# The first pair's first layer as 64-row halves from a list of slots, its setup and loads in another order

## The chip, the cores and the metric

The kernel runs on one core of a Trainium2 chip. The core has a matrix engine (PE, with weight loads shown apart as PEld), a vector engine (DVE), a scalar engine (ACT) and a general engine (POOL); SP only issues transfers. Each engine works through a queue of its own in the order in which the program issued its instructions, and semaphores make one engine wait for another. PE writes its products to PSUM, which has eight banks of 128 rows by 512 numbers. The metric is the device time of one execution in microseconds (us).

## The reference

It is a mixture of experts over 8 batches of 512 tokens with 256 features; all numbers are 32 bits wide.

```python
nx = layer_norm(x, ln_gamma, ln_beta)
weights = softmax((nx @ Wq) @ (ctx @ Wk)^T / 16)          # 64 prototypes of each batch
evidence = weights @ (ctx @ Wv)
combined = concat([nx, evidence, anchor])                 # 768 features; anchor is one row of a batch
router_probs = softmax(combined @ router_W + router_b)    # 3 experts
h = silu(combined @ e_w1 + e_b1)                          # 3 experts of 512
routed = sum over experts of (h @ e_w2 + e_b2) * router_probs
g = sigmoid(silu(combined @ gate_w1 + gate_b1) @ gate_w2 + gate_b2)
out = x + g * (routed @ out_w + out_b)
```

## The kernel before, in words

The batches are worked in four pairs (`j` = 0 to 3). The two batches of a pair and the two halves of the 256 features make 2 by 2 blocks, and the kernel forms block products by Strassen's scheme in Winograd's form: seven products in the place of eight. The sums of inputs are the tile `T` (`combine_x`), the sums of weights are `ws`, `w2s` and `gw2s` (`combine_weights`, `combine_second`, `combine_gate`, on POOL).

**Setup.** Context, weights and x are loaded by SP, ACT and POOL. PE transposes, joins the key weights, forms the values, and then the scores. DVE subtracts the maxima, ACT takes the exponential (line 679), DVE sums and divides and turns the weights (`turn_weights`). `value_weights` multiplies the values by an expert's evidence weights (`ps_vw`); ACT copies them out and `value_differences` subtracts. `anchor_rows` multiplies the anchors by an expert's anchor weights, in 32-column pieces; `anchor_columns` adds the biases (`abias`). `second_bias` does the same for the second layer's bias.

**First layer.** The first layer has seven groups of two 128-feature chunks: group 0 is the gate, groups 1 and 2 are expert 0, 3 and 4 expert 1, 5 and 6 expert 2. A group has the products P1 to P7 (`nx_operands`, line 881), collected in PSUM sums called U, Z and Y (and W for the gate). To these sums come evidence products of only 64 rows, since a batch has 64 prototypes; two of them, one on the upper and one on the lower 64 rows of PE, run side by side. A chunk is made in steps: ACT copies a sum out (`keep_part`, line 876), DVE adds another (`add`, line 873), ACT applies silu with the anchor's bias (line 867), and DVE multiplies by the router's probability (`weigh_chunk`, line 924, or subtracts, line 921).

**Order.** All queues are in program order (`manual_schedule(engines=None)`, line 1426). `gate_layer` issues P1, P5, P2, P6, P3 and P7 of the gate, with other steps put between. In pairs 1 to 3 `half_layers` then reads the list `SLOTS`. Each line is a slot: two half products, the first on the upper 64 rows and the second on the lower, and behind the bar the steps of the other engines that are issued after them. So every product is split in two halves that stand in different slots; `half_product` adds a semaphore wait where a bank goes from one half to the other. `HOME` gives the bank of each sum. In the steps, k is a copy out of PSUM, a an add, s a silu, w a weighing, df a difference, each with two digits for the chunk and the group behind the dot; st, nm and lg are statistics, normalization and router part of the next pair; r is the router with the spreading of its probabilities (`pb`, a round trip through memory); g is a gate difference.

In pair 0 the first layer runs in another way: `expert_layer` issues whole 128-row products of two groups at a time, and `evidence` issues the 64-row products in four blocks, behind the gate and behind each expert. Between them the lists `within` put steps that pair 0 alone has: the anchors of experts 1 and 2, the combined weights of experts 1 and 2, and the second layer's product of `e_w2` and `out_w`. For that, `transpose_second` turns one expert's `e_w2` (DVE) in scratch tiles that earlier held setup data, `second_layer` multiplies it by `out_w`, and `combine_second` forms its sums on POOL. `outputs` then does the gate's second layer, the expert sums and the stores, and prepares the next pair.

The helper `product` (line 809) records nearly all products, so PE's instructions are told apart by their tiles: `ps_u`, `ps_z`, `ps_y` and `ps_w` are the sums above; `ps_gu`, `ps_gz` and `ps_gy` are the gate's second layer. A 32-bit product is two PE instructions in the trace.

## Time and profile before

| | |
|---|---|
| median of 3 runs (lowest to highest) | 459.16 us (458.97 to 459.51) |
| profiled execution: its time, its span | 458.83 us, 457.0 us |
| PE busy | 451.6 us (99%) |
| DVE, ACT, POOL busy | 364.0, 214.6, 100.3 us |
| granted PE clock | 1.000 |
| PE in pair 0: first score product | starts at 19.30 us |
| PE in pair 0: first gate product of the outputs | starts at 95.36 us |

The span reaches from the first to the last instruction, and times inside the profile count from its start. A line of the timeline gives start, duration, engine, line of the program, operation, output and input tile, their shapes, the number of instructions, and in brackets the idle time of the engine just before with what seems to have ended it. Products overlap on PE, so that the distance of two starts says more than a duration. Where the engine named in the brackets had long been done, another one ended the wait.

### The profile page before, as it was taken

How to read it: one execution, taken by the hardware profiler on the slowest of the kernel's cores; microseconds unless marked ns; L12 is line 12 of the kernel's file. 1: busy time of each engine (PE TensorE's matmuls, PEld its weight loads, DVE VectorE, ACT ScalarE, POOL GpSimd, SP SyncE). 2: the span in 40 equal slices, each digit the busy share in tenths (PEclk: the TensorE clock that was granted, in tenths of full speed). 3: DMA queues.
4: the chain of work that ended last, by engine and by line, in shares of the span. 5: the costliest groups of instructions: out<-in, count | busy, mean ns of one | idle time of the engine just before them, and what ended most of it. 6: DMA issues, size and time to landing. Idle time of an engine off the chain costs nothing.

```text
span 457.0 us, 5304 instructions
## 1 busy us (share of the span) xinstructions
PE 451.6 (99%) x1711; PEld 212.8 (47%) x1711; DVE 364.0 (80%) x679; ACT 214.6 (47%) x373; POOL 100.3 (22%) x148
## 2 busy tenths in 40 slices
PE   9999999999999999999999999999999999999996
PEld 7534555444444444444444444444444444444445
DVE  2888979969699899479689999578869746677983
ACT  3545683655221585467221576468220456558000
POOL 5367715001072300001062300001044300000010
PEclk9999999999999999999999999999999999999999
DMA  8985587302011387303011377102011390000014
GB/s 266 384 163 125 94 241 123 91 0 46 7 23 25 58 241 129 81 0 48 6 23 23 48 226 126 19 0 47 6 23 23 55 223 3 0 0 1 0 17 75
DMA packets 119346, 35.30 MB, mean 77 GB/s; under 512 B 105980, under 2 KB 116280, under 8 KB 118808
## 3 DMA queue, kind: packets, MB, share of 16 engines
q1 hardware_dynamic: 115312, 27.02, 29.2%
q0 software_dynamic: 2080, 7.16, 4.7%
q10 hardware_dynamic: 1928, 0.80, 0.7%
q8 instruction: 13, 0.21, 0.2%
q14 instruction: 13, 0.11, 0.1%
HBM read 27.56 MB, written 7.39 MB: 76 GB/s over the span
## 4 chain that ended last, share of the span: by engine, by line
PE 97%; POOL 1%; issue 0%; DVE 0%; ACT 0%; POOLq 0%
PE ps_u L809 45%; PE ps_z L809 19%; PE ps_y L809 14%; PE ps_vw L782 5%; PE ps_gu L809 3%; PE ps_w2o L510 2%; PE ps_gz L809 2%; PE ps_s L660 1%; PE ps_tokens L809 1%; PE ps_wake L307 1%; PE ps_v L347 1%; PE ps_gy L809 1%; PE ps_m L347 1%; PE pt_ctx L326 0%; PE pt_x L590 0%; PE ps_kq L360 0%
## 5 line engine op out<-in xcount | busy, mean ns | idle before, releaser
L809 PE MATMUL ps_u<-nxT,w 64*128 64x512 f32 (+1 forms) x184 | 86.8, 591 | 0.0
L924 DVE TENSOR_TENSOR h<-h,pb 128x512 f32<-128x512 f32 x96 | 63.4, 698 | 14.8 <-ACT h L867 12.2
L809 PE MATMUL ps_u<-h,w2o 128*128 128x512 f32 x144 | 64.2, 595 | 0.0
L867 ACT ACTIVATE h<-h,abias 128x512 f32<-128x512 f32 x72 | 49.3, 718 | 24.4 <-DVE h L873 24.2
L809 PE MATMUL ps_z<-wT,vw 64*128 64x512 f32 x104 | 51.6, 593 | 0.0
L1331 POOL TENSOR_TENSOR yb<-yb,xb 128x512 f32<-128x512 f32 x14 | 17.7, 1267 | 148.9 <-DVE yb L1330 131.7
L809 PE MATMUL ps_z<-T,ws 64*128 64x512 f32 (+1 forms) x92 | 46.4, 590 | 0.0
L809 PE MATMUL ps_z<-nxT,ws 64*128 64x512 f32 (+1 forms) x92 | 45.9, 590 | 0.0
L809 PEld LDWEIGHTS ps_u<-nxT,w 64*128 64x128 f32 (+1 forms) x184 | 33.2, 188 | 26.9 <-issue 24.5
L809 PE MATMUL ps_y<-nxT,w 64*128 64x512 f32 (+1 forms) x92 | 45.5, 590 | 0.0
L809 PE MATMUL ps_u<-T,ws 64*128 64x512 f32 (+1 forms) x92 | 42.9, 590 | 0.7 <-POOL gg L412 0.7
L809 PE MATMUL ps_z<-h,w2s 128*128 128x512 f32 x96 | 42.5, 592 | 0.0
L809 PE MATMUL ps_u<-T,w 64*128 64x512 f32 (+1 forms) x98 | 42.4, 589 | 0.0
L809 PEld LDWEIGHTS ps_u<-h,w2o 128*128 128x128 f32 x144 | 27.0, 190 | 32.6 <-issue 30.4
L876 ACT COPY h<-ps_u 128x512 f32<-128x512 f32 x48 | 27.9, 582 | 24.1 <-PE ps_u L809 22.0
L1298 DVE TENSOR_TENSOR h<-h,h 128x1024 f32<-128x1024 f32 x24 | 34.3, 1485 | 0.0
L424 POOL DMA_DIRECT2D vrd<-vw x8 | 5.0, 628 | 133.2 <-ACT vw L789 128.9
L809 PEld LDWEIGHTS ps_z<-h,w2s 128*128 128x128 f32 x96 | 18.2, 190 | 23.0 <-issue 22.3
L809 PE MATMUL ps_y<-wT,vw 64*128 64x512 f32 x56 | 28.0, 596 | 0.0
L809 PE MATMUL ps_u<-wT,vw 64*128 64x512 f32 x56 | 27.9, 595 | 0.0
L782 PE MATMUL ps_vw<-w,vT 128*128 128x512 f32 (+1 forms) x64 | 26.9, 543 | 0.0
L873 DVE TENSOR_TENSOR h<-h,ps_u 128x512 f32<-128x512 f32 x24 | 16.1, 684 | 11.2 <-PE ps_u L809 11.1
(224 smaller groups left out, 814.3 us busy)
## 6 DMA issues: line engine op xcount, KB each, us to landing
pb<-pd POOLq DMA_DIRECT2D x4, 1536.0 KB, 6.5
xb<-in_x_dram SPq DMA_DIRECT2D x64, 64.0 KB, 2.4
out_dram<-yb SPq DMA_DIRECT2D x56, 64.0 KB, 2.0
w<-in_L_xcond_e_w_dram SPq DMA_DIRECT2D x6, 512.0 KB, 10.5
x<-in_x_dram SPq DMA_DIRECT2D x24, 128.0 KB, 2.8
xd<-x SPq DMA_DIRECT2D x24, 128.0 KB, 2.4
xg<-xd SPq DMA_DIRECT2D x48, 64.0 KB, 2.3
scr_wa<-in_L_xcond_e_w_dram SPq DMA_DIRECT2D x3, 512.0 KB, 17.4
```

Source lines behind the costliest of these rows:

```text
L307: nc.tensor.matmul(ps_wake[0][:, :P], zeros, zeros, start=True, stop=True)
L347: nc.tensor.matmul(ps, w_sb[:, k, m * P : (m + 1) * P], src[:, k, :], start=(k == 0), stop=(k == KH - 1))
L424: nc.gpsimd.dma_start(S["vrd", j][i].rearrange("e c -> c e"), S["vw", j][row_half(i), R0:])
L510: nc.tensor.matmul(ps[:, d * H : (d + 1) * H], w2T[:, k, (i + d) * P : (i + d + 1) * P], ow_sb[:, k, :], start=(k == 0), stop=(k == KH - 1),)
L782: nc.tensor.matmul(ps, vT[:, k, j * 2 * CT : (j + 1) * 2 * CT], w1[:, KH + k, n0:n1], start=(k == 0), stop=(k == KH - 1),)
L809: return nc.tensor.matmul(ps, lhsT, rhs, start=start, stop=True, skip_group_check=not start)
L867: nc.scalar.activation(h, h if src is None else src, AF.Silu, bias=abias[:, c, 2 * j + i : 2 * j + i + 1])
L873: nc.vector.tensor_tensor(h, h, part, ALU.add)
L876: nc.scalar.copy(chunk(n, i, d), part)
L924: nc.vector.tensor_tensor(h, h, S["pb", j][:, i, :, 2 * q // RC, :], ALU.mult)
L1298: nc.vector.tensor_tensor(d, p, m, ALU.subtract)
L1331: nc.gpsimd.tensor_tensor(yb, yb, S["xb", 2 * j + row][:, i, :], ALU.add)
```

## The change

Pair 0 uses `gate_layer` and `half_layers` like the others, with lists of its own: `SLOTS_0`, `UNITS_0`, `LATE_0` and `HOME_0`. The old way (`expert_layer`, `evidence`, `weigh` and what they call) is gone. In the lists `lp` is the router part of pair 0, `rl` its router logits, `rx` the exponential, `c2` and `cg` combine the weights of expert 2 and of the gate, `lx`, `l1` and `l2` issue loads, and `t` turns half of an expert's `e_w2`.

- The second layer's products stand behind the slots, in six units of half an expert; the transposed halves lie in two tiles, taken in turns. `e_w2` is loaded to tiles of the `xb`, `r11` and `r12` buffers in the place of scratch, and the load of expert 0 is issued in the setup.
- The anchors of all three experts and the second bias are one block of products to one bank (`late_anchors`), with one transpose, between `gate_layer` and the slots.
- `load_first` loads one part at a time: the evidence parts of all experts come ahead of the first parts of experts 1 and 2, and the anchor weights are loaded between.
- The gate's weights are combined before the first transposes of x; those of experts 0 and 1 behind the softmax, held back by a one-element copy on POOL (`wake_t`) that reads the softmax.
- `scores` is split: `exponents` (all behind the products) is issued after the gate's P1 and its copy. All four `combine_x` steps of pair 0 are on DVE. The three `ps_vw` products are inside `gate_layer`; the rest of the softmax is issued behind P7 and before its add.

```diff
-    def load_first(g):
+    def load_first(g, part):
         src, n = (e_w1[g], RH) if g < E else (gate_w1, H)
-        cs = slice(g * RH, g * RH + n)
-        nc.sync.dma_start(w1[:, KH:, cs], rows_of(src[H : 2 * H, :]))
-        nc.sync.dma_start(w1[:, :KH, cs], rows_of(src[:H, :]))
+        lo = part * KH
+        nc.sync.dma_start(
+            w1[:, lo : lo + KH, g * RH : g * RH + n], rows_of(src[part * H : (part + 1) * H, :])
+        )
...
+    def turned(ps, rows_of_k, weights, first):
+        for k in range(KH):
+            w = weights[:, k, :].rearrange("p (c i f) -> p i c f", i=P // QB, f=QB)
+            for i in range(P // QB):
+                dst = ps[i * QB : (i + 1) * QB, first : first + weights.shape[2] // (P // QB)]
+                nc.tensor.matmul(
+                    dst.rearrange("p (c f) -> p c f", f=QB), rows_of_k[:, k, :], w[:, i, :, :],
+                    start=(k == 0), stop=(k == KH - 1),
+                )
...
+    def late_anchors():
+        ps = bank(1, "ps_ar")
+        for g in range(E):
+            turned(ps, condT, wa[g], g * P)
+        turned(ps, b2T, ow_sb, E * P)
+        blocks = work.tile([P, T], F32, tag="yb", name="ar_blocks")
+        n = E * P + KH * QB
+        nc.vector.transpose(blocks[:, :n], ps[:, :n])
+        for g in range(E):
+            ar[g] = blocks[:, g * P : (g + 1) * P]
+        ar["b2"] = blocks[:, E * P : n]
...
+    def second_layer(u):
+        e, i = u // 2, 2 * (u % 2)
+        ps = bank((4, 7, 6, 5)[u % 4], f"ps_w2o_{u}")
+        for d in range(2):
+            for k in range(KH):
+                c = k * H + d * P
+                nc.tensor.matmul(
+                    ps[:, d * H : (d + 1) * H], w2["T"][u % 2][:, c : c + P], ow_sb[:, k, :],
+                    start=(k == 0), stop=(k == KH - 1),
+                )
+        c = e * RC + i
+        nc.scalar.copy(w2o[:, c : c + 2, :].rearrange("p c n -> p (c n)"), ps)
+        if i:
+            combine_second(e)
...
+            if t0 == 0:
+                S["ls", b] = work.tile([P, NT], F32, tag="ls", name=f"ls_{b}")
+            sums = S["ls", b]
         for t in range(t0, t1):
             nc.vector.scalar_tensor_tensor(
                 junk, S["xn", b][:, t, :], 1.0, gg, ALU.mult, ALU.mult, accum_out=sums[:, t : t + 1]
             )
-        if j == 0:
+        if j == 0 and t1 == NT:
...
+        S["ps_s", j] = ps
+    def exponents(j):
+        ps = S.pop(("ps_s", j))
...
+        def run(point):
+            for step in steps.get(point, ()):
+                step()
         for i in range(2):
             for k in range(KH):
                 S["hg", i, k] = hpool.tile([P, T], F32, tag=f"hg{i}{k}", name=f"hg_{2 * j + i}_{k}")
         U[n], Z[n], Y[n] = (bank(i, f"ps_{u}_{j}_{n}") for i, u in ((0, "u"), (2, "z"), (3, "y")))
         nx_product(j, n, 1, True)
         keep_part(n, 0, 0, U[n])
-        if j == 0:
-            anchor_columns(E)
-            anchor_columns(0)
...
+        run(1)
         nx_product(j, n, 5, True)
         keep_part(n, 1, 1, Z[n])
+        run(5)
         nx_product(j, n, 2, True)
         nx_product(j, n, 6)
         keep_part(n, 1, 0, U[n])
-        for step in steps.get("gate early", ()):
-            step()
+        run(6)
         nx_product(j, n, 3)
-        for step in steps.get("gate", ()):
-            step()
+        run(3)
         nx_product(j, n, 7)
+        run("sums")
...
+    SLOTS_0 = (
+        "P1.1 Z.1 |",
+        "Y.1 Z.0 |",
+        "P1.3 P1.1 | lp0.0 a10.0",
+        "Y.0 W.0 | k00.1 lp0.1 s10.0 lp0.2",
+        "P2.1 P1.3 | w11.0",
+        "P4.0 P5.1 | a00.0 k00.3 s11.0 lp0.3 c2",
+        "P6.1 P2.1 | lp1.0 s00.0 lp1.1",
+        "P5.1 Z.2 | a00.1",
+        "U.0 P6.1 | lp1.2 k11.1 lp1.3 cg lx l1 l2 s00.1",
+        "P1.2 P5.2 | rl k10.1",
+        "Y.2 P4.0 |",
+        "P5.2 P1.2 | s01.0",
+        "P2.3 P3.1 | k00.2 k11.2",
+        "P7.1 V.1 | g0 rx",
+        "P2.2 Z.3 | st0.0 st0.1",
+        "P6.2 P7.1 | st0.2 st0.3",
+        "Y.3 P5.3 | a11.1",
+        "P3.1 P6.2 | r s11.1",
+        "P6.3 V.2 | st1.0 k10.2 a10.1",
+        "P5.3 P3.2 | st1.1 s10.1",
+        "U.1 P2.2 | st1.2 k11.3 st1.3",
+        "P3.2 P2.3 | a00.2 dev",
+        "P1.6 P6.3 | g1 a00.3",
+        "P7.2 P3.3 | a10.2",
+        "P4.1 P1.6 | g2",
+        "P2.4 P7.2 | g3 k10.3 nm0.0 k00.6",
+        "P1.5 P4.1 | nm0.1 a11.2 s00.2",
+        "P1.4 V.3 | nm0.2 s01.1 nm0.3 xd0",
+        "P7.3 P1.5 | nm1.0 s00.3 nm1.1 nm1.2 s10.2",
+        "P3.3 P1.4 | nm1.3 xd1 xg w00.1 k00.5",
+        "P6.6 Z.6 | a10.3 k00.4",
+        "P4.2 P7.3 | s11.2 w10.1 w11.1 s10.3",
+        "U.2 P6.6 | a11.3",
+        "P6.5 Z.4 | k10.6 w00.2 s11.3 w01.1",
+        "P6.4 P4.2 | w00.3",
+        "Y.4 P6.5 | s01.2 w10.2",
+        "U.3 P6.4 | w11.2 k10.5 w10.3",
+        "P4.3 P2.4 | k10.4 w11.3",
+        "Y.6 P5.4 | a00.4 w01.2",
+        "P7.5 P4.3 | s00.4 lg0.0",
+        "P5.4 P5.6 | w00.4 s01.3 lg0.1",
+        "P7.4 Z.5 | k11.4 w01.3",
+        "P5.6 P5.5 | lg0.2 lg0.3",
+        "Y.5 P7.4 | lg1.0 k11.6 lg1.1",
+        "P5.5 P7.5 | lg1.2 a11.4",
+        "P2.5 P3.4 | k11.5 lg1.3 s11.4 df.1",
+        "P7.6 V.6 | a11.5 t0",
+        "P2.6 P3.6 | w11.4 s11.5",
+        "U.4 V.5 | df.2 w11.5",
+        "P3.6 P7.6 | df.3",
+        "U.5 P3.5 | a11.6 a10.6 t1",
+        "P4.5 V.4 | s11.6 s10.6 w11.6",
+        "P4.4 P2.5 | w10.6",
+        "U.6 P4.5 | a00.5",
+        "P4.6 P4.4 | s00.5 s01.5",
+        "P3.4 P2.6 | w00.5 s01.4 w01.5",
+        "P3.5 P4.6 | a00.6",
+    )
+    UNITS_0 = (
+        "a10.4 s01.6 s10.4",
+        "t2 a10.5 s00.6",
+        "w01.4 t3 s10.5 xb0 xb1",
+        "w01.6 w00.6 t4",
+        "w10.4 t5",
+        "w10.5",
+    )
+    LATE_0 = ("", "", "df.6 df.4 df.5")
+    HOME_0 = {
+        "U.0": 0, "Z.0": 2, "Y.0": 3, "W.0": 1, "U.1": 4, "Z.1": 5, "Y.1": 6, "U.3": 7, "Z.2": 2,
+        "U.2": 1, "Y.2": 3, "Y.3": 6, "Z.3": 0, "U.6": 5, "Y.4": 3, "U.5": 6, "U.4": 2, "Z.6": 4,
+        "Z.4": 0, "Y.6": 1, "Z.5": 3, "Y.5": 7,
+    }
...
+            "rl": lambda: router_logits(j),
+            "rx": lambda: router_exp(j),
+            "c2": lambda: combine_weights(2),
+            "cg": lambda: combine_gate(),
+            "lx": lambda: [load_x(b) for b in (2, 3)],
+            **{f"l{e}": lambda e=e: load_second(e) for e in range(1, E)},
+            **{f"t{u}": lambda u=u: transpose_second(u) for u in range(2 * E)},
...
+        if not j:
+            for u, tokens in enumerate(UNITS_0):
+                second_layer(u)
+                for token in tokens.split():
+                    step(token)
+        S["late", j] = [lambda t=tokens: [step(x) for x in t.split()] for tokens in late]
...
-        for g in (E, 0):
-            load_first(g)
-            load_anchor(g)
-        for g in (1, 2):
-            load_first(g)
+        load_first(E, 1)
+        load_first(E, 0)
+        load_anchor(E)
+        load_first(0, 1)
+        load_first(0, 0)
+        load_first(1, 1)
+        load_first(2, 1)
+        load_anchor(0)
...
+        combine_weights(E)
         transpose_x(0)
+        late_scratch()
+        load_anchor(1)
+        load_anchor(2)
+        nc.sync.dma_start(ow_sb, rows_of(out_w))
+        load_first(1, 0)
+        load_first(2, 0)
+        nc.sync.dma_start(gw2_sb, rows_of(gate_w2))
+        load_second(0)
...
-        combine_weights(E)
         load_table(AF.Exp)
         combine_x(0, nc.vector, (0, 1))
+        spares(6, 4, 5, 7)
         scores(0)
-        anchor_rows(0)
-        combine_x(0, nc.gpsimd, (2,))
-        router_column()
-        spread_router_bias()
-        combine_weights(0)
-        spread_router_rows(0)
-        value_weights(0, 0, nc.scalar.copy, False)
-        sum_weights(0)
-        softmax(0)
-        value_differences(0, 0)
-        turn_weights(0)
-        late_scratch()
-        load_anchor(1)
-        load_anchor(2)
-        nc.sync.dma_start(ow_sb, rows_of(out_w))
-        nc.sync.dma_start(gw2_sb, rows_of(gate_w2))
-        load_second(0)
+        def begin_softmax():
+            exponents(0)
+            combine_x(0, nc.vector, (2,))
+        def end_softmax():
+            sum_weights(0)
+            softmax(0)
+            nc.gpsimd.tensor_copy(wake_t, S["w", 0][:, 0, 0, 0:1])
+            value_differences(0, 0)
+            turn_weights(0)
+            anchor_columns(E)
+            combine_x(0, nc.vector, (3,))
+            combine_weights(0)
+            router_column()
+            spread_router_bias()
+            spread_router_rows(0)
+            combine_weights(1)
+        def end_setup():
+            value_differences(0, 1)
+            late_anchors()
+            for g in range(E):
+                anchor_columns(g)
+            value_differences(0, 2)
+            second_bias()
...
+            spares(7, 5)
             if j == 0:
+                spares(4, 5, 7)
+                copies = []
+
+                def value_product(g):
+                    value_weights(0, g, lambda *args: copies.append(args), False)
+
+                def copy_values():
+                    nc.scalar.copy(*copies.pop(0))
+
+                put(within, 1, value_product, 0)
+                put(within, 1, begin_softmax)
+                put(within, 5, copy_values)
+                put(within, 6, load_table, AF.Silu)
+                put(within, 3, value_product, 1)
+                put(within, 3, copy_values)
+                put(within, "sums", end_softmax)
+                put(within, 7, value_product, 2)
+                put(within, 7, copy_values)
+                put(within, 7, end_setup)
...
-            if j:
-                half_layers(j)
-            else:
-                for e in range(E):
-                    expert_layer(j, e, within)
+            half_layers(j)
             outputs(j, between)
```

## Prediction

> **What bounds the kernel now.** I read the busy times first, then the chain that ended last, then TensorE's own timeline of the first pair, and only then the queues of the other engines.
>
> ```profile
> span 457.0 us, 5304 instructions
> PE 451.6 (99%) x1711; PEld 212.8 (47%) x1711; DVE 364.0 (80%) x679; ACT 214.6 (47%) x373; POOL 100.3 (22%) x148
> PE 97%; POOL 1%; issue 0%; DVE 0%; ACT 0%; POOLq 0%
> ```
>
> TensorE (PE) is the chain. The clock row is 9 in all 40 slices, so nothing is to be had there. A change helps only if it takes products or gaps out of PE's queue, and it harms as soon as another engine makes PE wait. PE's timeline of the first pair shows what gaps there are:
>
> ```profile
> 25.12 1.02 PE L809 MATMUL ps_y<-nxT,w 128*128 128x512 f32 x2
> 26.82 1.10 PE L809 MATMUL ps_u<-T,ws 128*128 128x512 f32 x2 [0.68 <-POOL gg L412]
> ...
> 30.33 1.02 PE L809 MATMUL ps_u<-nxT,w 128*128 128x512 f32 x2
> 31.29 0.69 PE L809 MATMUL ps_y<-wT,vw 64*128 64x512 f32 x1
> ...
> 31.82 0.59 PE L809 MATMUL ps_y<-wT,vw 64*128 64x512 f32 x1
> ...
> 34.39 0.59 PE L809 MATMUL ps_y<-wT,vw 64*128 64x512 f32 x1
> ...
> 34.92 1.13 PE L809 MATMUL ps_u<-nxT,w 128*128 128x512 f32 x2
> 35.88 1.02 PE L809 MATMUL ps_u<-T,w 128*128 128x512 f32 x2
> ```
>
> Starts matter here, not durations, because products overlap. A full product is two instructions and takes 0.857 us (35.88 to the next start, 36.74); a pair of 64-row halves takes 0.429 an instruction, so 0.857 as well. Halves are therefore no faster in themselves. What costs is the border between the two shapes: 30.33 to 31.29 is 0.96, not 0.857, and 31.29 to 31.82 is 0.53, not 0.43. That is 0.1 on either side, 0.2 a border; 34.39 to 34.92 (0.53) and 34.92 to 35.88 (0.96) say the same of the way back. The first pair goes to halves and back four times: eight borders, 1.6 us. Pairs 1 to 3, which run the list of slots, have two each.
>
> The gap at 26.82 is put down to gg, but no operand of that product (P6 of the gate) is gg. It adds into bank ps_u, which ScalarE (ACT) has to read first, and ACT's queue shows when it did:
>
> ```profile
> 25.13 0.63 ACT L679 ACTIVATE w<-w 128x512 f32<-128x512 f32 x1 [4.00 <-DVE w L678]
> 25.67 0.57 ACT L789 COPY vw<-ps_vw 128x512 f32<-128x512 f32 x1
> 26.14 0.59 ACT L876 COPY hg<-ps_u 128x512 f32<-128x512 f32 x1
> ```
>
> The copy stood behind the softmax's exponential, ended at 26.73, and PE went on at 26.82. P2 was issued out at 25.98, so PE lost 0.84.
>
> **The change, part by part.** Account: PE from the first score product (19.30) to the first gate product of the outputs (95.36), 76.06 us. Work in it: scores 1.73, anchors 0.56 + 1.23, three ps_vw 5.16, 63 products and pairs of halves 54.0, second layer 10.35: 73.0. The rest, 3.0, is borders 1.6, the ACT wait 0.84, and some 0.6 of single gaps (0.25 behind the anchors, 0.19 in the third second-layer block).
>
> *Products.* All 57 first-layer products and evidence pairs stay, now as 57 slots; the 24 second-layer products stay, in six units of 1.72 (half of a 3.45 block). No work goes. Borders fall from eight to two: **-1.2**.
>
> *ACT order.* The copy of ps_u is issued ahead of the exponential, so P6 is free: **-0.84**. What is late next: the copy of ps_z is now behind the exponential. ACT 25.67 + 0.59 = 26.26, and P3 would start at 26.2 to 26.35: **+0.1**.
>
> *Anchors together*, second bias with them, as one block of the same 64 instructions: gap of 0.2 at one place instead of two, **-0.2**.
>
> *Loads on SP, DMAs on POOL.* SP moves load_anchor(0) behind two more weight loads, takes the first-half loads of experts 1 and 2 behind ow_sb, and sends the eight DMAs of load_second(0) at some 19 to 24 instead of 30.5, where SP stood 11.2 us on a scratch tile. DMA is busy to about 26 now; the moved loads of 512 KB are first read at 34 or later: nothing, up to +0.5 if the 64 KB DMAs delay them. POOL combines the gate weights before the router column's two DMAs, which go out at 16, not 14.2; 6.1 us to landing is 22, needed at 30: nothing. The wake copy holds POOL until the softmax is done (27.45); behind it are combine(0) 2.75, gg 1.8, four DMAs 2.15 and combine(1) 2.75: 37.2. P2 of expert 0 reads combine(0) (30.4) in slot 5 at 37; covered.
>
> *Start of the slots.* PE: scores to 21.03, six gate products 5.15, three ps_vw 5.15, anchors 1.8, borders 0.3: slot 1 at **33.5**. DVE: softmax as before to 30.5, then 0.2 + 0.6 + 0.6 + 0.4, then the anchors' transpose at 33.5 (0.65), columns 0.35, difference 0.4, second bias 1.06: its first slot step at **36.1**, in slot 3, where it is listed.
>
> *DVE's ledger.* From 36.1 to the last transpose before unit 5 the lists put on DVE: 21 adds and 23 weighings and 3 differences at 0.60 (28.2), 16 router parts at 0.44 (7.0), router logits 3.93, router 0.85, eight statistics at 0.53 (4.2), eight normalizations (3.1), four gate differences (2.6), six half transposes at 0.74, worked out between 0.30 for 128 columns and 0.71 for 512 (4.4): **54.3**. PE reaches unit 5 at 33.5 + 0.1 + 48.9 + 8.6 = 91.1, so 55.0 are there: **slack 0.7**. Before, the same engine idled 7.9 of 64.1:
>
> ```profile
> 31.30:95.40 64.10, 64.10 (x244) 31.97 (x243) 56.23 (x134) 36.79 (x59) 28.90 (x54) 1.00 0.58 126
> ```
>
> (Columns: stretch, its length, then busy time of PE, PE loads, DVE, ACT and POOL.) So each idle microsecond of DVE beyond 0.7 comes back as a PE wait. I find three:
> - Router logits wait for POOL's copies of the second batch's sums, queued behind combine(2). First batch's copies end at 40.8, + 2.73 = 43.6, + 2.2 = 45.8; DVE is there at 44.9: 0.9. Bounds: 0 and 1.9. Behind it on DVE stand a gate difference, statistics and the add that frees bank 4 for slot 21.
> - The first weighing waits for the probabilities. From router to their landing was 50.78 to 55.79 and 6.5: 11.5. DVE's work between the two steps in the list is 11.4: 0.1. In pair 2 the way took 6.1 + 7.0 = 13.1: up to 1.7.
> - Single waits on ACT near the end, 1.0 as an allowance, from 0 to 2.
>
> Sum 2.0, less 0.7: **+1.3**.
>
> *Contention.* combine_second now runs beside weighings in the units. That happened once before:
>
> ```profile
> 76.33 2.95 DVE L924 TENSOR_TENSOR h<-h,pb 128x512 f32<-128x512 f32 x3
> 79.31 1.10 DVE L921 TENSOR_TENSOR h<-h,h 128x512 f32<-128x512 f32 x1
> ...
> 76.64 0.95 POOL L245 TENSOR_TENSOR w2s<-w2o 128x256 f32<-128x256 f32 x1 [4.12 <-ACT w2o L515]
> ```
>
> Three in 2.95 is 0.98 each, not 0.60; POOL's own step took 0.95, against 0.74 at 56.38. Three weighings fall beside combine_second(0): 0 to 1.15. I take **+0.4**, since one of them stands right ahead of a transpose for which PE has no time to spare. [...]
>
> Sum: -1.2 - 0.84 - 0.2 + 0.1 + 1.3 + 0.4 = **-0.45**. What follows the first gate product has the same instructions, except that DVE weighs less there; no change. The profiled execution took 458.83 (span 457.0 and 1.83 around it); it would take 458.4. The median shown, 459.16, is 0.33 above it: **458.7**.
>
> **Rivals.**
> - *The lists hold, faster.* POOL's copies come in time and DVE's waits stay within the slack, as in pairs 1 to 3, where not one slot waits. PE then keeps +0.1 to +0.5 of waits: -2.24 + 0.3 = -1.95, **457.2**. For: 57 slots at 0.857 in the later pairs. Against: there DVE is busy 47.3 of 56.1, here 54.3 of 55.0.
> - *POOL beside DVE, slower.* Place: combine(2) beside router parts and logits, combine_second beside the units. Price 0.38 for each of two router products and four weighings (2.3) and 0.2 for three router parts (0.6): 2.9 in the place of the 0.4, so +2.05: **461.2**. It decides from 0.85 on, some three slowed instructions.
> - *The wait changes its place, no change.* The P6 wait comes back at P3 in full (0.84 for 0.1), the rest as in the forecast: +0.3, **459.5**.
>
> **How the numbers follow.** Measurement can tell about 0.2%, 0.9 us (458.24 to 460.08). The forecast (0.28) and the moved wait (0.10) lie within: 0.38 for no change. The lists hold: 0.36, faster. POOL beside DVE or late probabilities (13.1 for 11.5): 0.26, slower. All of the gain without waits would be 456.8; both slow terms together pass 462. For 8 in 10 the range is 457.0 to 461.0; the likeliest case alone is 458.3 to 459.9.
>
> **What would show it.** Right: eight borders become two; no gap at P6; slots start near 33.5; the first gate product at 94.9. The router logits' last steps show a wait on POOL's copies, the first weighing one on the probabilities, and PE waits near slots 21 to 24 and 34 and in units 2 to 4. Wrong: no PE wait after slot 1 (then 457.2), or weighings of 0.98 beside POOL in the units and a first gate product behind 96.3. A slot 1 behind 35 would mean that a load or POOL came late, which I priced at nothing.

## The result and the profile after

| | before | changed |
|---|---|---|
| median (lowest to highest, executions) | 458.9 us (458.78 to 459.51, 6) | 463.5 us (462.49 to 464.76, 6) |
| profiled execution: time, span | 458.83, 457.0 | 463.15, 460.8 |
| first gate product, counted from the first score product | 76.06 | 80.34 |

The ratio is 1.0099, 95% interval 1.0081 to 1.0117: 4.6 us slower, where 0.45 faster was forecast. The page of the changed kernel, span, busy time and granted clock:

```profile
span 460.8 us, 5500 instructions
...
PE 452.3 (98%) x1797; PEld 217.2 (47%) x1797; DVE 364.4 (79%) x683; ACT 214.1 (46%) x373; POOL 99.5 (22%) x148
...
PEclk9999899999999999999999999999999999999999
...
PE 87%; DMA 6%; POOL 3%; DVE 1%; issue 1%; SPq 0%; DVEq 0%; POOLq 0%
```

The chain is no longer PE alone: 6% of it is a transfer, 3% POOL. PE's timeline shows a good beginning:

```profile
24.61 1.02 PE L836 MATMUL ps_y<-nxT,w 128*128 128x512 f32 x2
25.47 1.02 PE L836 MATMUL ps_u<-T,ws 128*128 128x512 f32 x2
26.33 1.02 PE L836 MATMUL ps_z<-nxT,ws 128*128 128x512 f32 x2
...
33.24 0.69 PE L836 MATMUL ps_u<-nxT,w 64*128 64x512 f32 x1
```

P2, P6 and P3 stand 0.86 apart, so the gap at P6 is gone, and slot 1 starts at 33.24 (33.5 was forecast). Twenty slots later PE stands still:

```profile
50.08 0.59 PE L836 MATMUL ps_z<-T,ws 64*128 64x512 f32 x1
50.09 0.59 PE L836 MATMUL ps_z<-nxT,ws 64*128 64x512 f32 x1
54.46 1.22 PE L836 MATMUL ps_u<-wT,vw 64*128 64x512 f32 x1 [3.78 <-DVE h L878]
```

Slot 21 waits for DVE's add `a11.1`. DVE's timeline shows why the add was late:

```profile
46.06 0.69 DVE L752 TENSOR_REDUCE le<-pv 128x8 f32<-128x512 f32 x1
49.71 0.18 DVE L755 TENSOR_TENSOR lg<-lg,rbias 128x16 f32<-128x16 f32 x1 [2.97 <-POOL lg L643]
...
53.72 0.69 DVE L878 TENSOR_TENSOR h<-h,ps_u 128x512 f32<-128x512 f32 x1 [0.19 <-issue]
...
65.62 0.69 DVE L915 TENSOR_TENSOR h<-h,pb 128x512 f32<-128x512 f32 x1 [0.17 <-DMA pb<-pd]
```

The router logits stood 2.97 us for POOL's copies; a gate difference, four statistics and the add are queued behind them. POOL's timeline leads back to the first cause:

```profile
26.16 0.44 POOL L1484 COPY wake_t<-w 128x1 f32<-128x1 f32 x1 [4.59 <-DVE w L730]
32.29 0.63 POOL L248 TENSOR_TENSOR ws<-w 128x256 f32<-128x256 f32 x1 [5.70 <-DMA w<-in_L_xcond_e_w_dram]
...
38.74 0.83 POOL L248 TENSOR_TENSOR ws<-w 128x256 f32<-128x256 f32 x1
...
41.98 2.78 POOL L643 COPY lg<-ls 32x2 f32<-32x2 f32 x8
44.84 0.63 POOL L248 TENSOR_TENSOR ws<-w 128x256 f32<-128x256 f32 x1
...
47.95 1.73 POOL L643 COPY lg<-ls 32x2 f32<-32x2 f32 x8
```

Behind the wake copy POOL stood 5.70 us for a transfer. It then had a queue without a gap: combined weights of expert 0, router column, four issues, weights of expert 1, first copies, weights of expert 2 (44.84), and only then the copies that DVE waited for. The transfer is the last of the moved weight loads, `load_first(2, 0)`. The list of the chain (start, duration, what) has it from 15.45 to 32.14:

```profile
15.45 16.69 DMA w<-in_L_xcond_e_w_dram
```

`combine_weights(0)` reads only expert 0's weights, but it stood until this load of expert 2's had landed; the first parts of all three experts lie in one tile, `w1`. Last, windows around the gap, with the granted clock in the third column from the right:

```profile
50.50:54.46 3.96, 0.18 (x3) 0.00 (x1) 3.63 (x12) 2.81 (x4) 1.61 (x3) 0.82 0.77 123
54.46:60.20 5.74, 5.74 (x14) 2.89 (x16) 5.50 (x17) 4.30 (x8) 2.70 (x6) 0.53 0.14 22
60.20:99.57 39.37, 39.37 (x184) 24.23 (x181) 36.87 (x80) 23.09 (x37) 5.88 (x7) 1.00 0.49 114
```

After the standstill PE ran 5.7 us at 0.53 of its clock: a slot took 1.71 instead of 0.857.

### The profile page after: what moved, and what is told of

It is laid out like the page before. It is cut to its first block, busy times and chain, and to the rows that moved or that the text cites. A ratio compares the mean times of both kernels' runs of the same rounds, so it can differ in the third digit from the quotient of the medians.

```text
span 460.8 us, 5500 instructions
## 1 busy us (share of the span) xinstructions
PE 452.3 (98%) x1797; PEld 217.2 (47%) x1797; DVE 364.4 (79%) x683; ACT 214.1 (46%) x373; POOL 99.5 (22%) x148
## 4 chain that ended last, share of the span: by engine, by line
PE 87%; DMA 6%; POOL 3%; DVE 1%; issue 1%; SPq 0%; DVEq 0%; POOLq 0%
PE ps_u L836 42%; PE ps_z L836 19%; PE ps_y L836 12%; DMA w<-in_L_xcond_e_w_dram 5%; PE ps_vw L811 4%; PE ps_gu L836 3%; PE ps_w2o L541 2%; PE ps_gz L836 1%; DMA x<-in_x_dram 1%; PE ps_s L685 1%; PE ps_tokens L836 1%; POOL lg L643 1%; PE ps_gy L836 1%; POOL ws L249 1%; POOL ws L248 0%
## 5 line engine op out<-in xcount | busy, mean ns | idle before, releaser
L836 PE MATMUL ps_u<-nxT,w 64*128 64x512 f32 (+1 forms) x208 | 97.4, 595 | 0.0
L836 PE MATMUL ps_y<-nxT,w 64*128 64x512 f32 (+1 forms) x104 | 53.3, 609 | 0.0
L836 PE MATMUL ps_z<-nxT,ws 64*128 64x512 f32 (+1 forms) x104 | 53.1, 599 | 0.0
L836 PE MATMUL ps_z<-T,ws 64*128 64x512 f32 (+1 forms) x104 | 50.5, 589 | 0.0
L836 PEld LDWEIGHTS ps_u<-nxT,w 64*128 64x128 f32 (+1 forms) x208 | 37.6, 190 | 26.4 <-issue 23.8
L836 PE MATMUL ps_u<-T,ws 64*128 64x512 f32 (+1 forms) x104 | 49.5, 598 | 0.0
L836 PE MATMUL ps_u<-T,w 64*128 64x512 f32 x112 | 48.5, 589 | 0.0
L836 PE MATMUL ps_u<-wT,vw 64*128 64x512 f32 x56 | 29.1, 609 | 3.8 <-DVE h L878 3.8
L836 PEld LDWEIGHTS ps_z<-nxT,ws 64*128 64x128 f32 (+1 forms) x104 | 19.9, 192 | 13.4 <-issue 10.8
```

Source lines behind the costliest of these rows:

```text
L836: return nc.tensor.matmul(ps, lhsT, rhs, start=start, stop=True, skip_group_check=not start)
```

## The experiments

My theory: the late load holds POOL, POOL holds the router logits, DVE is late from there, and PE pays at slot 21 and then once more by the half clock (2.7 us). Rivals: POOL's queue is too long in any case; the transfers of `e_w2` make the load late; the half clock has another cause or no price. The ratio compares each run with the kernel before in the same session. That kernel's own median lay between 458.52 and 459.23 us in these sessions, so across runs the ratios say more than the medians.

| run | median us | ratio to before (95%) |
|---|---|---|
| w2_late | 463.88 | 1.0101 (1.0087 to 1.0114) |
| first_ahead | 461.91 | 1.0063 (1.0051 to 1.0075) |
| c2_behind | 461.71 | 1.0055 (1.0042 to 1.0069) |
| three | 460.90 | 1.0050 (1.0036 to 1.0064) |
| pb_early | 459.23 | 1.0009 (1.0000 to 1.0018) |
| w_behind | 459.59 | 1.0018 (1.0009 to 1.0026) |
| bias_late | 460.32 | 1.0041 (1.0022 to 1.0060) |
| all_five | 457.43 | 0.9974 (0.9965 to 0.9982) |
| load_back | 459.20 | 0.9998 (0.9989 to 1.0007) |
| fill | 463.82 | 1.0115 (1.0093 to 1.0137) |
| fill_w_behind | 463.00 | 1.0081 (1.0066 to 1.0096) |
| w_lg | 462.79 | 1.0089 (1.0070 to 1.0109) |
| fill_w_lg | 462.72 | 1.0074 (1.0052 to 1.0095) |
| act_back | 457.77 | 0.9983 (0.9974 to 0.9992) |
| no_wake | 457.42 | 0.9975 (0.9965 to 0.9985) |
| units_ahead | 457.04 | 0.9966 (0.9955 to 0.9978) |
| pool_early | 456.90 | 0.9951 (0.9938 to 0.9965) |
| pool_act_back | 457.42 | 0.9964 (0.9952 to 0.9977) |

### The late load

**w2_late**

```diff
-        load_second(0)
...
-        "U.0 P6.1 | lp1.2 k11.1 lp1.3 cg lx l1 l2 s00.1",
+        "U.0 P6.1 | lp1.2 k11.1 lp1.3 cg lx l0 l1 l2 s00.1",
```

> The changed kernel, but the eight loads of expert 0's e_w2 (64 KB each, rows of 128 bytes) are issued with those of experts 1 and 2 behind the x loads of the next pair, not in the setup. Theory 'small packets': they share the transfer engines with the last load of first-layer weights (expert 2, issued at 15.45, landed at 32.14), so without them it lands at 26 to 27, combine_weights(0) starts at 27 on POOL, the router logits do not wait, PE has no gap at slot 21 and its clock stays at 1.00: 463.5 - 3.9 - 2.7 = 456.9, up to 458.2 if DVE's queue is late at single slots. Rival 'place in the queue': the load is late because it stands behind two anchor loads and out_w; then combine_weights(0) still starts at 31 to 32 and the time stays at 462.5 to 464.5.

POOL's timeline of this run:

```profile
31.99 0.63 POOL L248 TENSOR_TENSOR ws<-w 128x256 f32<-128x256 f32 x1 [5.27 <-DMA w<-in_L_xcond_e_w_dram]
```

Hardly anything moved (12.6 us behind the first score product, where it was 13.1). The small packets are not the cause; the place in the queue is. The windows of this run (last two columns: busy share of the transfer engines, GB/s) show how the last load ends:

```profile
22.00:24.00 2.00, 2.00 (x6) 0.87 (x5) 1.82 (x6) 0.68 (x2) 0.00 (x0) 1.00 1.06 370
26.00:28.00 2.00, 2.00 (x6) 0.95 (x5) 1.89 (x5) 1.34 (x3) 0.44 (x1) 1.00 0.62 132
28.00:30.00 2.00, 2.00 (x6) 0.86 (x5) 1.94 (x5) 1.34 (x3) 0.00 (x0) 1.00 0.54 126
30.00:32.00 2.00, 2.00 (x17) 0.76 (x19) 1.15 (x3) 0.19 (x1) 0.01 (x1) 1.00 0.18 64
```

The bulk is through at 25, at some 370 GB/s; then the queue has a tail of six microseconds at a third of the rate and less. (In the changed kernel itself, with the small packets in it, the tail runs at 118 to 169 GB/s.) Before the change the tail was there too (124 GB/s from 26 to 28), but the anchor weights and `out_w` stood in it, which were read at 44 and later.

**first_ahead**

```diff
         load_first(2, 1)
+        load_first(1, 0)
+        load_first(2, 0)
         load_anchor(0)
...
         nc.sync.dma_start(ow_sb, rows_of(out_w))
-        load_first(1, 0)
-        load_first(2, 0)
```

> The changed kernel, but the first-part weights of experts 1 and 2 are issued ahead of the anchor weights, as before the change; e_w2 of expert 0 stays in the setup. Theory 'late load': combine_weights(0) waits for the last of these loads, which then lands at 22 to 25; it starts at 26.7 behind the wake copy, no gap at slot 21: 456.9 to 458.2. Rival 'POOL is too long in any case': the router logits still wait 2 us or more on POOL's copies and the time stays above 461. Rival 'anchors late': the anchors land behind 31.4 and late_anchors makes PE wait ahead of slot 1, 458 to 461.

```profile
26.89 0.63 POOL L248 TENSOR_TENSOR ws<-w 128x256 f32<-128x256 f32 x1
```

POOL starts 5.4 us earlier, with no wait, yet the time falls by 1.6 us only, and the range that I gave fails. DVE still stood 0.91 for POOL's copies and 1.79 for the probabilities; PE stood 1.57 at slot 21 and 1.31 at slot 34. The anchors made no wait. The rival of POOL's long queue has the time right, above 461, but not the wait, which it put at 2 us or more.

**c2_behind**

```diff
-        "P4.0 P5.1 | a00.0 k00.3 s11.0 lp0.3 c2",
+        "P4.0 P5.1 | a00.0 k00.3 s11.0 lp0.3",
...
-        "U.0 P6.1 | lp1.2 k11.1 lp1.3 cg lx l1 l2 s00.1",
+        "U.0 P6.1 | lp1.2 k11.1 lp1.3 c2 cg lx l1 l2 s00.1",
```

> The changed kernel, but combine_weights(2) is issued behind POOL's copies of the second batch's sums, so the router logits no longer stand behind it; loads as changed, combine_weights(0) still starts at 32 to 32.5. Theory 'gap, then clock': the copies end at 46.9 instead of 49.7, the gap at slot 21 falls from 3.9 to 1.1 us, and a gap that short leaves PE's clock at 1.00: 463.5 - 2.8 - 2.7 = 458.0. Rival 'the clock falls for another reason, or in proportion to the gap': the clock is still below 0.9 behind slot 21 and the time is 460 to 461. Rival 'another wait': P1 of group 6 or another step waits for combine_weights(2), 459 to 462.

The copies ended at 46.9 and the clock stayed at 1.00 in the profiled execution, as expected, with 0.79 of waiting at slot 21 (two of the other five executions have a mean clock of 0.996). But 1.8 us came back, not 5.5: PE now stood 0.84 at slot 34, behind a DVE that stood 1.33 for the probabilities. My sum counted gap and half clock as if nothing waited behind them.

**three** (these three edits together)

> All three edits together: e_w2 of expert 0 later, first-part weights ahead of the anchors, combine_weights(2) behind the copies. If the late load was the whole of the loss: first gate product at 95.36 - 2.2 = 93.2 and 456.6 to 457.0. If DVE's ledger is as tight as predicted (54.3 of 55.0 us): waits of PE of 1.3 us near slots 21 to 24 or in units 2 to 4, 458.0. If the e_w2 loads now come late for the first transpose (t0), a gap in unit 0, 459 or more.

No wait at slot 21 any more, no gap in unit 0, and still 460.9. All of it sits at one place now, in DVE's and in PE's timeline:

```profile
59.62 1.38 DVE L593 TENSOR_SCALAR x<-x,mv,rstd 128x256 f32<-128x256 f32 x4
63.50 0.69 DVE L915 TENSOR_TENSOR h<-h,pb 128x512 f32<-128x512 f32 x1 [2.50 <-DMA pb<-pd]
64.11 0.68 DVE L878 TENSOR_TENSOR h<-h,ps_z 128x512 f32<-128x512 f32 x1
```

```profile
64.84 0.69 PE L836 MATMUL ps_z<-wT,vw 64*128 64x512 f32 x1 [2.01 <-DVE h L878]
```

The first weighing waits for the probabilities; the add `a10.3` behind it frees the bank for slot 34. That is the wait that the prediction bounded by 1.7.

### The late probabilities and DVE's queue

**pb_early** (on three)

```diff
-        "U.0 P6.1 | lp1.2 k11.1 lp1.3 c2 cg lx l0 l1 l2 s00.1",
+        "U.0 P6.1 | lp1.2 k11.1 lp1.3 c2 lx l0 l1 l2 s00.1",
...
-        "P2.2 Z.3 | st0.0 st0.1",
-        "P6.2 P7.1 | st0.2 st0.3",
-        "Y.3 P5.3 | a11.1",
-        "P3.1 P6.2 | r s11.1",
+        "P2.2 Z.3 | st0.0 st0.1 r cg",
+        "P6.2 P7.1 |",
+        "Y.3 P5.3 | a11.1 st0.2 st0.3",
+        "P3.1 P6.2 | s11.1",
```

> Run three, but the router and its spreading stand behind two of the four statistics instead of behind four and an add (the other two go behind that add), and combine_gate stands behind them on POOL. In three the probabilities landed at 63.4, DVE waited 2.5 us for them, PE stood 2.9 us at slot 34 and its clock fell to half for 3.8 us. Theory 'late probabilities': they now land at 61.4 to 61.9, DVE waits 0.5, PE stands under 1 us, its clock stays 1.00: 460.9 - 2.0 - 1.9 = 457.0. Rival 'the transfer is the limit' (it runs beside the loads of e_w2 and the stores of the next x): landing stays at 63 or later and the time at 460 or more.

(Expectations here count PE's standstill in three as 2.9, the distance of two starts; its row says 2.01.) 1.7 us came back of 3.9. The spreading was issued 1.3 us earlier, but the transfer took 8.6 us instead of 7.8, and DVE still stood 1.61. Half of the theory, half of the rival: the transfer took 8.6 us here, beside 0.39 MB of loads and stores, and 6.4 alone (all_five).

**w_behind** (on three)

```diff
-        "P3.3 P1.4 | nm1.3 xd1 xg w00.1 k00.5",
+        "P3.3 P1.4 | nm1.3 xd1 xg k00.5",
...
-        "P4.2 P7.3 | s11.2 w10.1 w11.1 s10.3",
-        "U.2 P6.6 | a11.3",
+        "P4.2 P7.3 | s11.2 s10.3",
+        "U.2 P6.6 | a11.3 w00.1 w10.1 w11.1",
```

> Run three, but the first three weighings stand behind the adds a10.3 and a11.3, so DVE's wait for the probabilities no longer holds a PSUM bank. The probabilities land as in three (63 to 63.5). Theory 'the bank behind the weighing': PE does not stand at slot 34, its clock stays 1.00: 460.9 - 2.6 - 1.9 = 456.4. Rival 'DVE's ledger': DVE still loses its 2 us, and the wait of PE comes back at a later add (a00.4, a11.6) or in the units: 457.5 to 459. Rival 'no effect': PE still waits there, 460.9.

The wait at slot 34 is gone, and 0.74 of waiting appears some eight us later at another add. 459.59 is even above the range of the rival 'DVE's ledger'. What DVE loses, PE pays at a later bank.

**bias_late** (on three: `second_bias` behind the last unit, its 64 columns transposed to a tile of their own)

> Run three, but the second bias (1.0 us on DVE) is worked out behind the last second-layer unit, from a transposed piece of its own (0.2 us added ahead of the slots). Theory 'DVE is late from slot 1 on': all DVE steps to the first weighing come some 0.8 us earlier, the router and so the probabilities too; PE stands 2.0 us instead of 2.9 at slot 34, which leaves the clock at 1.00: 460.9 - 0.8 - 1.9 = 458.2. Rival 'only the transfer counts': no change, 460.5 to 461.

DVE came 0.6 us earlier and stood 3.34 instead of 2.50 for the probabilities, which landed at 63.6 (63.4 in three), since their transfer now took 8.6 us. PE stood 2.31. The work that went is waiting now, as the rival says; the 0.6 us less lie at the edge of the two intervals. Both runs hold executions with and without half clock: their mean spans are 458.6 without and 459.7 with it in three (three each), 457.8 and 459.9 here (five and three). This is not shown to be a price, since a longer standstill could make both. In c2_behind it is the other way round, 459.0 with it (two) and 459.55 without (four).

**all_five** (three and the last three edits, and the loads of `e_w2` of experts 1 and 2 behind the regrouping)

```diff
-        "P3.3 P1.4 | nm1.3 xd1 xg k00.5",
+        "P3.3 P1.4 | nm1.3 xd1 xg l1 l2 k00.5",
```

> Run three with all of it: router ahead, combine_gate behind it, first weighings behind the adds, second bias at the end, and the loads of e_w2 of experts 1 and 2 behind the regrouping of the next x. If late loads, late probabilities and DVE's start are the whole loss, PE has no wait over 0.5 us in the slots: first gate product at 93.2 to 93.7 and 456.5 to 457.0. If the ledger of 54.3 of 55.0 us is the bound, PE waits 0.5 to 1.5 us at late slots or in the units: 457.5 to 458.5.

```profile
61.26 0.68 DVE L879 TENSOR_TENSOR h<-h,ps_z 128x512 f32<-128x512 f32 x1
61.85 0.68 DVE L879 TENSOR_TENSOR h<-h,ps_u 128x512 f32<-128x512 f32 x1
62.45 1.89 DVE L916 TENSOR_TENSOR h<-h,pb 128x512 f32<-128x512 f32 x3
```

With no other transfer beside it the probabilities took 6.4 us, the weighing does not wait, and PE has no wait in any slot. 457.43 is faster than both kernels, and between the two ranges of the forecast. The rest of DVE's ledger is seen in the units, where the fifth and sixth block come 0.33 and 0.16 late for their transposes.

**load_back** (all_five with the change's order of the first loads)

> Run all_five (457.4) with the change's order of loads put back: the first-part weights of experts 1 and 2 behind the anchors and out_w. Theory 'the late load starts the chain, the lists decide what it costs': combine_weights(0) starts at 31 to 32 again, POOL's copies end near 46.9, the router logits wait 1 to 2 us, PE waits under 1.5 us: 458.0 to 459.0. Rival 'the late load is the loss': 460.5 or more, as the changed kernel. Rival 'no price': 457.4, the wait is hidden once the probabilities hold no bank.

`combine_weights(0)` starts at 31.72 again, the router logits wait 0.70, and the time is 459.20, just past the end of the theory's range. Against all_five that is 1.8 us by the medians, 1.1 by the ratios and 1.3 in the profiled executions. So the late load alone costs 1 to 2 of the 6 us that lie between the changed kernel and all_five, as in first_ahead, where mending it gave back 1.6; the lists behind it make the rest of it.

### The half clock

**fill**

```diff
+        "D.3 E.2 |",
+        "D.3 E.2 |",
+        "D.3 E.2 |",
+        "D.3 E.2 |",
         "U.1 P2.2 | st1.2 k11.3 st1.3",
...
+            if kind in "DE":
+                half_product((U if kind == "D" else Z)[n][: QB - B, :], condT[rows, 0, B:], S["nxT", 2 * j][rows, 0, :], k)
+                return
```

> The changed kernel itself, with four slots of products with zeros added ahead of slot 21 (16 PE instructions of 64 rows, 3.4 us; they add zero to two open banks, so the output is the same). They run while PE would stand there for DVE's late add; the late load and DVE's wait stay as they are. Theory 'the idle time halves the clock': with 0.5 us idle left in the place of 3.9, the clock stays 1.00 and the time falls by the price of the half clock, 463.5 - 2.7 = 460.8. Rival 'the clock falls with the load of the other engines or the transfers': it falls all the same, 463.5. Rival 'the products cost': the DVE wait is shorter than thought, 463.5 or more.

Windows of this run, the gap filled, the slots behind it, and slot 34:

```profile
50.60:54.65 4.05, 4.05 (x21) 0.77 (x17) 3.65 (x14) 3.18 (x4) 1.34 (x2) 1.00 0.73 116
54.65:65.80 11.15, 11.15 (x53) 7.21 (x53) 10.09 (x28) 10.11 (x17) 2.71 (x6) 1.00 0.50 165
65.80:68.39 2.59, 1.13 (x6) 0.19 (x2) 1.34 (x3) 0.02 (x1) 0.00 (x0) 1.00 0.75 190
```

Half of the theory holds: here it was PE's idle time that halved the clock, since with DVE as late as ever and PE kept busy it stays at 1.00, in five of six executions (0.999 to 1.000; the sixth has 0.995, for a reason that is not known). The price was wrong: the time did not fall. PE reached slot 34 earlier and stood there 1.5 us for the probabilities, for which DVE waited 2.06. Part of that is the transfer, which took 8.0 us here and 6.4 in the changed kernel.

**fill_w_behind** (fill with the edit of w_behind)

> Run fill (the changed kernel, zero products in PE's idle time at slot 21, output the same) with the first three weighings behind the adds a10.3 and a11.3. In fill the clock stayed at 1.00 and the time did not fall: PE then stood 2.0 us at slot 34 for the probabilities (landed at 66.9). Theory 'two delays side by side': the half clock in the changed kernel fills time in which PE would wait for the probabilities anyway; with both out of the way at slot 34 the time falls, by 2.0 if nothing follows, by 1.0 to 1.5 if DVE's late weighings hold a later bank: 461.8 to 462.8. Rival 'PE is late for another reason': 463.5 to 464.

463.00, 0.8 less than fill by the medians and 1.6 by the ratios, whose intervals still overlap. The theory wanted 1.0 to 2.0, so it is neither shown nor refuted. PE's waits spread over later adds, with DVE idle 6.1 us from slot 1 to the last transpose.

**w_lg and fill_w_lg** (the changed kernel with the edit of w_behind and the next pair's router parts behind the units; then with the zero products too)

```diff
-    LATE_0 = ("", "", "df.6 df.4 df.5")
+    LATE_0 = ("", "lg0.0 lg0.1 lg0.2 lg0.3 lg1.0 lg1.1 lg1.2 lg1.3", "df.6 df.4 df.5")
```

> The changed kernel with two reliefs of DVE behind the gap at slot 21: the first three weighings stand behind the adds a10.3 and a11.3, and the eight router parts of the next pair (3.5 us on DVE) behind the last second-layer unit. The late load, the gap at slot 21 and the half clock behind it stay. Theory 'two bounds side by side': in the changed kernel PE has no wait behind slot 21, it needs 37 slots, 10.4 us of units and 2.7 us of half clock from 54.46, 99.3; relief of DVE alone gains nothing: 463.0 to 463.5. Rival 'DVE alone': 463.5 - 2.5 = 461.0 or less.

> Run w_lg with the zero products of run fill in PE's idle time at slot 21, so the clock stays at 1.00 (output the same). Theory 'two bounds side by side': the half clock was the only bound that w_lg left behind slot 21, so the time falls by its price, to 463.2 - 2.7 = 460.5; in fill, where DVE was not relieved, the same products gained nothing. Rival 'the half clock is free in any case': as w_lg, 463.0 to 463.5.

462.79 and 462.72. Relief of DVE alone gains little (0.7 by the medians), against the rival. Between the two runs no price of the half clock can be seen, and the intervals would hide 1 us and more. In the profiled executions the way from the router logits to the first gate product is 48.9 with half clock and 47.9 without, which speaks for about 1 us; the start of that way, set by the load, moved by as much between executions. For the changed kernel the 2.7 are refuted; what lies between 0 and 1 stays open.

### The other steps

**act_back** (all_five, the exponential ahead of the copy as before the change)

```diff
         nx_product(j, n, 1, True)
-        keep_part(n, 0, 0, U[n])
         run(1)
+        keep_part(n, 0, 0, U[n])
```

> Run all_five with one part of the change undone: the softmax's maxima and its exponential are issued ahead of the copy of the gate's P1 again. Step of the prediction under test: that order is worth 0.84 at P6, less 0.1 at P3. Theory: ACT's copy waits behind the exponential again and PE stands 0.7 to 0.85 us ahead of P6: 457.4 + 0.75 = 458.2. Rival 'hidden': PE is held at the same point by something else (P5's sums, the three ps_vw), 457.4.

P6 follows P2 without a gap here too, and the time is as without the edit (457.77 and 457.43, intervals overlap). DVE's timeline of this run tells why:

```profile
23.48 0.69 DVE L708 TENSOR_TENSOR w<-w,mx 128x512 f32<-128x512 f32 x1
```

Before, the same subtraction took 1.68 us (23.42, line 678), while POOL worked on `combine_x` and the router column beside it. POOL is quiet there now, the exponential comes 1.3 us earlier (counted from the first score product), and the copy is in time in either order.

**pool_early and pool_act_back** (all_five with `combine_x`'s third step and the router column on POOL beside the softmax; then with act_back's edit too)

```diff
-            combine_x(0, nc.vector, (2,))
+            combine_x(0, nc.gpsimd, (2,))
+            router_column()
...
             combine_weights(0)
-            router_column()
```

> Run all_five with POOL busy beside the softmax as before the change: the third step of combine_x on POOL and the router column ahead of the wake copy; ACT's order as changed (copy ahead of the exponential). Before the change DVE's subtraction of the maxima took 1.68 us there, now 0.69. Theory 'the order protects P6, not P3': the subtraction takes 1.2 to 1.7, the exponential ends up to 1 us later, P6 does not wait, P3 waits 0 to 0.3: 457.4 to 457.7. Rival 'POOL idle is the gain': PE waits 0.5 or more: 457.9 or more.

> Run pool_early with the exponential issued ahead of the copy as well, so both are as before the change. In act_back, with POOL quiet, that order alone cost nothing at P6. Theory 'only both together make the gap': the subtraction takes 1.2 to 1.7, the copy ends 0.5 to 1.0 later than in act_back and P6 waits 0.4 to 0.8: 457.4 + 0.6 = 458.0. Rival 'neither': no gap, 457.4 to 457.8.

With both undone the gap at P6 is back, 0.32 of it (PE's timeline of pool_act_back: P2 at 24.67, the next start 1.18 later):

```profile
24.67 1.02 PE L837 MATMUL ps_y<-nxT,w 128*128 128x512 f32 x2
25.85 1.10 PE L837 MATMUL ps_u<-T,ws 128*128 128x512 f32 x2 [0.16 <-issue]
```

The subtraction took only 0.83 to 0.93 in these two runs, under the forecast, since POOL's step of `combine_x` was over before it began; and the gap is smaller than the 0.84 of before. The time shows no clear price: 457.42 is what the rival 'neither' gave, and its ratio and that of pool_early have overlapping intervals. pool_early, the order kept and POOL's work early, has the lowest median, 456.90, below its forecast. There `combine_weights(1)` starts 0.9 us earlier than in all_five, counted from the first score product, and DVE's three additions for the anchors take 1.15 us instead of 1.95; which of the two gives the time was not tested.

**no_wake**

```diff
-            nc.gpsimd.tensor_copy(wake_t, S["w", 0][:, 0, 0, 0:1])
```

> Run all_five without the one-element copy that holds POOL until the softmax is done, so combine_weights(0) starts as soon as its loads have landed, beside DVE's softmax. Theory 'hidden': POOL gets up to 2 us earlier, DVE's softmax steps up to 1 us each slower beside it, but DVE stands 1.9 us for the anchors' products anyway: 457.2 to 457.6. Rival 'POOL beside DVE': the softmax gets over 2 us later, DVE's steps in the slots too, PE waits again at slots 21 or 34: 458 to 460.

457.42: hidden, as expected. POOL started at 23.0, DVE's third step of `combine_x` took 1.21 beside it (0.68 in act_back).

**units_ahead**

```diff
-        "w01.4 t3 s10.5 xb0 xb1",
-        "w01.6 w00.6 t4",
-        "w10.4 t5",
+        "t3 w01.4 s10.5 xb0 xb1",
+        "t4 w01.6 w00.6",
+        "t5 w10.4",
```

> Run all_five, with the transposes t3, t4 and t5 issued ahead of the weighings of the same unit. In all_five PE stood in the last two units for t4 and t5, which were 0.33 and 0.16 us late behind weighings. Theory 'DVE's ledger': the units shrink from 10.96 to 10.4, 457.4 - 0.5 = 456.9. Rival 'given back in outputs': the weighings are late there instead, 457.4.

457.04, the theory's 0.5 less, though the intervals of the two runs overlap. In the profiled execution the first gate product stands 73.93 behind the first score product, where all_five had 74.80.

## Why the prediction was wrong, step by step

*What bounds the kernel.* PE was named as the chain, and a second engine as the danger: right. "The clock row is 9 in all 40 slices, so nothing is to be had there" overlooked that there was something to be lost.

*Products, ACT order, anchors.* The three gains less P3 came to 2.14. They could be had: units_ahead, in which no wait of PE is listed in the slots, is at 73.93, which is 2.13 below 76.06. As a sum they were right; one by one they were not measured, and P3 paid nothing (0.86 behind P6 in the changed kernel) where 0.1 was put. The reason given for the 0.84 was incomplete: the order was one of two conditions and POOL beside the softmax the other, since the order alone makes no gap (act_back), and both together make 0.32 of it (pool_act_back).

*Loads on SP, DMAs on POOL: the step that failed.* The prediction said: "the moved loads of 512 KB are first read at 34 or later: nothing, up to +0.5". They are waited for at 27, by `combine_weights(0)`, though it reads nothing of theirs, and the last of them landed at 32.14, 16.7 us after its issue. "DMA is busy to about 26 now" was read off the bulk; the queue's tail goes on to 32, and the change put a load there on which POOL's whole queue stands. `combine_weights(0)` came at 32.3, not 27.5, and POOL's last copies ended at 49.7, not 45.8. This step alone is less than half of the 4.8 us between forecast and result: with the load mended, 1.6 came back (first_ahead). With the other two edits of run three as well, 460.9 is still 2.2 above the forecast, and the wait that is left there is the one for the probabilities.

*Start of the slots.* 33.24 for 33.5. DVE's first slot step came at 37.25 for 36.1: the anchors' columns took 1.56 for 0.35, beside POOL. The check "a slot 1 behind 35 would mean that a load or POOL came late" looked at the wrong place: PE's start does not read POOL's late results, slot 21 does.

*DVE's ledger.* The mechanism was right and is the real account of the result. From the anchors' transpose to the last transpose of the units, windows of the changed kernel and of all_five (third of the busy times is DVE):

```profile
33.38:97.65 64.27, 60.49 (x268) 32.96 (x269) 58.50 (x143) 35.95 (x57) 24.35 (x48) 0.95 0.48 103
```

```profile
33.74:92.77 59.03, 58.96 (x269) 37.88 (x270) 57.09 (x140) 35.92 (x58) 20.63 (x40) 1.00 0.53 115
```

In fifteen of the nineteen profiled executions with the changed lists the first gate product follows the end of DVE's last transpose by 1.6 us (1.61 to 1.63). In the changed kernel, in run three, in w_lg and in fill_w_lg it is 1.9, so the transpose has 0.3 to spare there, and PE is the bound by that much. Within that, the time is DVE's work plus DVE's idle time. Forecast were 2.5 for the setup steps and 54.3 of work, 56.8, plus 2.0 idle and 0.4 of contention; measured are 58.5 of work and 5.8 idle (1.9 of them in all_five too). That is 5.1 more; the distance to the first gate product is 4.7 above the forecast. The term that was mis-sized most is the idle time, by 3.8: the router logits waited 2.97, put at 0.9 with a bound of 1.9, because POOL was late, and some 1.7 lie in gaps under 0.2 us that the ledger left out. The other 1.3 is work: 1.7 more of it, less the 0.4 that was put for contention. Two of its pieces stand beside POOL and above their forecast: the anchors' columns (1.2 more) and the weighings in the units (see below).

*Probabilities.* From router to landing the prediction took 11.5, with 13.1 as a bound. Changed kernel: 54.32 to 65.45, 11.1. Once the load was mended it was 13.2 (three: 50.16 to 63.4), because the transfer ran beside other loads and stores (7.8 us for 6.4) and POOL stood 0.7 longer ahead of it; the wait of 0.1 became 2.5, past its bound of 1.7.

*Contention.* DVE's timeline of the changed kernel in the units, beside `combine_second`:

```profile
93.36 1.79 DVE L915 TENSOR_TENSOR h<-h,pb 128x512 f32<-128x512 f32 x2
95.07 0.76 DVE L531 STREAM_TRANSPOSE w2T<-w_r 128x256 f32<-128x256 f32 x2
95.76 1.21 DVE L915 TENSOR_TENSOR h<-h,pb 128x512 f32<-128x512 f32 x1
```

A weighing takes 1.21 instead of 0.60, and two of them stand ahead of the last transpose: 1.2, where +0.4 was taken and 1.15 was the bound. The loss of 0.61 is somewhat less than one of POOL's instructions there (0.72 to 1.18), and more than the 0.38 of the row that the sum went by.

*Rivals and range.* "POOL beside DVE or late probabilities" named both engines and 461.2; its mechanisms are there, but POOL's lateness, not its neighbourhood, made most of it. That "both slow terms together pass 462" was seen and left outside the range, and no case let two terms meet that depend on one load. So the range ended at 461.0, 2.5 below the result.

## What to carry to other kernels

When loads are put in another order, ask of the last one in the queue who waits for it, and for the whole tile, not for the part that is read (`combine_weights(0)` stood 5.70 us for expert 2's part of `w1`); its landing was the end of the queue's tail here, 32.14, not of its bulk, 25. Where two engines both have under a microsecond to spare, a wait that is taken away can show the next one (in three, 2.50 us for the probabilities): add up work and idle time of the second engine up to the last thing that the first needs, instead of adding up the first one's gaps. A gap or a half clock that stands in the trace need not have a price of its own, since something later may have waited anyway (fill kept the clock at 1.00 and took 463.82 for 463.5); fill it before counting on it.

## What the runs showed of the hardware

- In the profiled execution of the changed kernel PE stood for 3.78 us; its clock was 1.00 up to 52.8, some 2 us into the gap, and 0.50 from 53.2 to 59.6, so that the 5.7 us behind the gap ran at 0.53. w2_late (a gap of 3.69, then 0.62 from 54.51 to 59.00) and w_lg (4.17, then 0.64 from 57 to 60) show the half clock too, and all executions of these three have a mean clock of 0.991 to 0.996. A gap of 2.01 us was followed by half clock in the profiled execution of three (0.56 from 65.80 to 69.65), one of 2.31 us in that of bias_late was not (1.00); by the mean clock (0.992 to 0.996) it fell in three of six and three of eight executions of these runs. In c2_behind, with waits of 0.8 in the profiled execution, two of six had 0.996; how long PE stood in those is not known. With the clock down, PE worked for 3.4 (w_lg) to 5.7 us until it was back at 1.00. The length of the gap alone does not tell in these runs whether the clock falls; what else decides was not shown.
- Products with zeros, 24 columns wide, kept the clock at 1.00 in five of six executions of fill and all six of fill_w_lg.
- The queue of loads ended in a tail: from 370 GB/s to 118 to 169 with small packets in it (changed kernel) and to 64 to 132 without (w2_late), for six us; the last two 512 KB loads took 16.7 and 15.0 us from issue to landing (medians).
- The same 1.5 MB spreading of the probabilities took 6.4 us alone (all_five), and 6.4 to 8.6 beside loads of 64 KB or the stores of x: 6.4 where these moved 0.11 MB meanwhile (changed kernel), 8.0 with 0.38 MB (fill), 8.6 with 0.39 and 0.89 MB (pb_early, bias_late).
